# One graph layer with routed experts: an earlier closing of open blocks, an earlier first combine, the routing three slots sooner, and 112 block places

## The chip, the cores and the metric

The kernel runs on one core of a Trainium2 chip. Its time is device microseconds from start to end of one launch; the median of three runs is 1729.33 us (1729.07 to 1730.34). A separate execution was recorded by the hardware profiler. All durations of instructions come from that one.

The core has a matmul engine (PE, with its weight loads shown as PEld), three engines for elementwise work (DVE, ACT, POOL) and SP, which here only issues DMAs. Each engine works through its own instructions in program order. DMAs issued by SP form one ordered list of issues, and the indirect DMAs (gathers and scatters by a list of row numbers) are issued by POOL.

## The reference

Input: 6250 nodes with 256 features, 100000 edges sorted by destination, 16 experts. All float32.

```
xn  = layernorm(x)
gnn: h = xn @ W; deg = segment_sum(ew, dst) + 1; dinv = rsqrt(deg)
     agg = segment_sum(dinv[src]*ew*dinv[dst] * h[src], dst) + dinv^2 * h + b
     gnn = relu(0.5*(layernorm(agg)*gamma + beta) + 0.5*xn)
mix: q, k = elu(xn Wq^T)+1, elu(xn Wk^T)+1;  v = xn Wv^T      (8 heads of 32)
     mix = (q (k^T v) / max(q . sum(k), 1e-6)) Wproj^T + bproj
x   = x + gnn + mix
ffn: z = layernorm(x); top 2 of 16 experts by z @ gate_w + gate_b; softmax of the two
     moe = sum over the two of w * (relu(z @ w1[e] + b1[e]) @ w2[e] + b2[e])
x   = x + layernorm(z + moe)*gamma2 + beta2
```

So every node is sent to two experts: 12500 rows for the expert network, whose weights are 512 KB (w1) and 512 to 642 KB (w2 with biases) for one expert.

## The kernel before

**Tiles and slots.** The nodes form `NT` = 49 tiles of 128. X stays in SBUF. The order of the work is written by a loop over *slots* at the end of `windowed_layer`. Slot `c` (0 to 781) issues the gather of the 128 source rows of edge chunk `c` (line 1269, POOL), builds its one-hot matrix `hot` (line 1273, DVE), and six slots later (`LAG`) multiplies the two on PE (line 1282). All other work is cut into generators. `weave.add(at, piece)` puts one into a queue by slot, `yield n` puts the rest of it n slots later. A slot is thus a place in the program order of every engine, not a time.

**What is woven in, in this order.** `attend(t)` computes the attention's sums (slots up to 159). `residual` of a tile pair follows its edges: it finishes the two branches, updates X and computes the routing logits, over 20 slots. After each group of tiles in `PHASES`, `route(a, b, lo, hi, ...)` picks the two experts of each token, gives each token a row ("slot") in `xslots`, and lists the blocks of 128 rows that are now full. `scatter` then writes the normalised tokens to `xslots` (line 974, POOL, two scatters a tile; the norms are ACT's at line 963, in four places named `token`). Each listed block becomes one `expert` piece: SP loads w1, the block's rows and w2; PE transposes (line 1045), first product (1055), second product (1065); DVE or ACT adds the bias; SP stores the block to `yslots`. `sync` at line 1002 is the issuer of nearly all these DMAs.

**Blocks not yet full.** An expert's last block is open until it fills. At one phase (`part`) the open blocks that this phase did not fill up are closed and listed although they are not full. In the last phase `close` lists all remaining open blocks, in the order in which they were opened. The pieces of blocks are fixed in the program: `hi` says how many blocks are listed after each phase, `USUAL` how many in all. Which expert and which rows a block has is read from the list at run time (the `rows` registers on SP).

**The combine.** `combine` takes two tiles: POOL gathers four times 128 rows from `yslots` (line 1111), ACT normalises X again (1120), DVE weighs and adds (1127), takes the statistics (319, 320), normalises (1135) and adds X (1138, or 1140 and 1141 where the sum with beta was not prepared by `shift`, line 1096); SP stores the output. `LIMITS` holds pairs (tile, block): tiles below the first number have all their rows in blocks below the second, so the gather waits for the store of that block and not for all stores. The combine of a pair is placed no sooner than the slot where that block's store stands (`stored_at`).

**The guard.** `usual` is multiplied by a test at each listing: at least `hi` blocks are full, at most `FIRST` after the closing, and each pair of `LIMITS` and `USUAL` hold. If it ends at zero, the last part of the program (`again`) runs all blocks and combines once more.

**Places.** Buffers in SBUF are lent by `Places`: `spare(t)` is Q's tile t, free once the residual has read it (`read`). `got` (14 places) holds gathered rows, `w1` and `w2` have four places each, `more` holds the sums of `shift`.

The slot arithmetic of the kernel before gives, around its end: the last gather at slot 781; the residuals of the last three tiles from slots 781 and 791; routing of the last phase from 815; listed blocks 81 to 87 from slots 799 to 823 in steps of four; the last 26 blocks, 88 to 113, from slots 829 to 929; combines from slot 835 (tiles 0 and 1) in steps of five to 958.

## Time and profile before

| what | value |
|---|---|
| median of three runs | 1729.33 us |
| profiled execution, its own time | 1475.86 us |
| its span, first to last instruction | 1473.9 us |
| mean granted TensorE clock | 0.942 |
| busy: PE, PEld, DVE, ACT, POOL | 1245.1, 986.9, 914.2, 513.2, 965.5 us |
| gathers of edge rows (line 1269) | 782, 971 ns each |
| scatters of tokens (line 974) | 98, 1026 ns each |
| gathers of expert rows (line 1111) | 98, 1015 ns each |
| last gather of edge rows is issued at | 1217.5 us |
| first and last gather for the combine | 1299.2 and 1454.3 us |
| last store of a block is issued at | 1443.4 us |
| bytes moved | 353.71 MB, mean 240 GB/s |

The profiled execution is 253.5 us shorter than the median. Its span and its own time differ by 2 us. A row of the profile names line, engine, operation, and written and read tiles. "PE busy" counts modelled ends of pipelined matmuls. In tables of stretches each row gives the stretch, its length, busy time and number of instructions of each engine, the granted clock, the share of DMA time and the rate of bytes.

### The profile page before, as it was taken

Reading aid. Unit: us, or ns where it says so; the run is one execution under the profiler, and the core shown is the slowest. Engines: PE = TensorE matmul, PEld = TensorE weight load, DVE = VectorE, ACT = ScalarE, POOL = GpSimd, SP = SyncE. Lnnn points to the kernel's source line nnn. Section 1 sums busy time; section 2 is a strip of 40 time slices with the busy share of each in tenths; the row PEclk is TensorE's granted clock in tenths of the full one; section 3 lists DMA queues with packets and bytes.
Section 4 is the critical chain, followed back from the end, with each engine's and each line's share of the span. In section 5 each row is a group of like instructions: output and inputs, shape, how many; then the busy total and the mean of one; then the engine's idle time right before and its main releaser. Section 6 shows DMA issues by size and latency. Waiting matters only on the chain. (4 is left out here: it accounts for less than half of the span.)

```text
span 1473.9 us, 24429 instructions
## 1 busy us (share of the span) xinstructions
PE 1245.1 (84%) x6958; PEld 986.9 (67%) x6958; DVE 914.2 (62%) x3277; ACT 513.2 (35%) x1379; POOL 965.5 (66%) x999
## 2 busy tenths in 40 slices
PE   4879999989967787989989899797988998977880
PEld 3836666666645676877778787686867886866760
DVE  8853444457977474575745657465565456578885
ACT  3753344433332232322223232232332333345551
POOL 1007777777767777777777777777777773167634
PEclk9999999998977999999999899998999999999995
DMA  9879943333334677767878687787777887989993
GB/s 272 295 235 375 384 148 97 104 99 110 109 105 159 226 241 253 268 226 265 269 245 269 226 269 262 241 282 233 234 241 250 285 284 255 310 279 386 376 325 106
DMA packets 176777, 353.71 MB, mean 240 GB/s; under 512 B 26753, under 2 KB 115876, under 8 KB 176626
## 3 DMA queue, kind: packets, MB, share of 16 engines
q1 hardware_dynamic: 128646, 222.97, 43.7%
q0 software_dynamic: 47712, 128.17, 27.5%
q8 instruction: 62, 1.02, 0.3%
q10 hardware_dynamic: 268, 0.82, 0.2%
q14 instruction: 89, 0.73, 0.1%
HBM read 277.46 MB, written 74.38 MB: 239 GB/s over the span
## 5 line engine op out<-in xcount | busy, mean ns | idle before, releaser
L1269 POOL DMA_INDIRECT rows<-w_hs,src_t x782 | 759.6, 971 | 335.5 <-issue 92.3
L1282 PE MATMUL acc<-rows,hot 128*128 128x256 f32 x1564 | 445.4, 401 | 69.6 <-DMA rows<-w_hs,src_t 58.3
L1282 PEld LDWEIGHTS acc<-rows,hot 128*128 128x128 f32 x1564 | 278.9, 198 | 138.7 <-issue 56.1
L1273 DVE TENSOR_SCALAR hot<-iota_g,loc_t,w_t 128x128 f32<-128x128 f32 x782 | 244.7, 354 | 15.0 <-PE acc L1282 14.4
L974 POOL DMA_INDIRECT w_xslots<-Q,slot_i x98 | 100.5, 1026 | 77.6 <-ACT hT L1061 39.0
L1065 PE MATMUL yp<-early,hT 128*128 128x256 f32 x592 | 142.4, 384 | 2.2 <-ACT hT L1061 2.2
L1111 POOL DMA_INDIRECT Q<-w_yslots,slot_i x98 | 99.5, 1015 | 65.6 <-DVE xn L1127 20.1
L1061 ACT ACTIVATE hT<-hp,early 128x128 f32<-128x128 f32 x296 | 84.2, 367 | 160.5 <-PE hp L1055 116.8
L1055 PEld LDWEIGHTS hp<-Q,early 128*128 128x128 f32 x992 | 124.3, 199 | 6.2 <-ACT Q L1049 3.3
L1055 PE MATMUL hp<-Q,early 128*128 128x128 f32 x992 | 126.6, 283 | 2.1 <-ACT Q L1049 1.9
L1065 PEld LDWEIGHTS yp<-early,hT 128*128 128x128 f32 x592 | 111.8, 192 | 18.5 <-ACT hT L1061 3.7
L1049 ACT COPY Q<-xtp 128x256 f32<-128x256 f32 x114 | 42.1, 369 | 212.4 <-PE xtp L1045 211.1
L1291 DVE SCALAR_TENSOR_TENSOR agg<-acc,dinv,agg 64x256 f32<-64x256 f32 x135 | 65.1, 482 | 76.2 <-PE acc L1282 73.2
L1055 PE MATMUL hp<-Q 128*128 128x128 f32 x832 | 107.7, 286 | 0.1
L1055 PEld LDWEIGHTS hp<-Q 128*128 128x128 f32 x832 | 105.6, 202 | 2.7 <-ACT Q L1049 0.5
L569 DVE SCALAR_TENSOR_TENSOR row<-two_a,two_b 128x256 f32<-128x256 f32 (+1 forms) x49 | 21.0, 429 | 132.3 <-ACT two_b L567 132.3
L563 PE MATMUL kq<-early,xnT 128*128 128x512 f32 (+1 forms) x196 | 98.3, 625 | 4.4 <-ACT xnT L559 4.4
L1074 DVE TENSOR_TENSOR Q<-yp,early 128x256 f32<-128x256 f32 x61 | 25.8, 423 | 112.9 <-PE yp L1065 112.7
L1065 PE MATMUL yp<-Q,hT 128*128 128x256 f32 x320 | 78.3, 388 | 3.2 <-ACT hT L1061 3.2
L325 ACT ACTIVATE sd<-mv,eps_t 128x2 f32<-128x2 f32 (+2 forms) x76 | 22.7, 299 | 160.7 <-DVE mv L320 155.0
L566 ACT ACTIVATE two_a<-kq 128x512 f32<-128x512 f32 (+1 forms) x49 | 29.3, 597 | 119.3 <-issue 92.6
L1065 PEld LDWEIGHTS yp<-Q,hT 128*128 128x128 f32 x320 | 60.6, 195 | 12.8 <-ACT hT L1061 4.8
(302 smaller groups left out, 1810.5 us busy)
## 6 DMA issues: line engine op xcount, KB each, us to landing
early<-in_experts SPq DMA_DIRECT2D x61, 642.0 KB
early<-in_experts SPq DMA_DIRECT2D x62, 512.0 KB
Q<-in_experts SPq DMA_DIRECT2D x52, 512.0 KB
Q<-in_experts SPq DMA_DIRECT2D x27, 642.0 KB
w_xslots<-zero_b SPq DMA_DIRECT2D x16, 1024.0 KB
w_yslots<-zero_b SPq DMA_DIRECT2D x16, 1024.0 KB
Q<-w_xslots SPq DMA_DIRECT2D x114, 128.0 KB
w_yslots<-Q SPq DMA_DIRECT2D x114, 128.0 KB
```

The lines of the kernel that those rows point to most:

```text
L563: nc.tensor.matmul(kq[:r], xnT[:, k, :r], wkq[:, k, :], start=(k == 0), stop=(k == 1))
L566: act(e[:r].rearrange("p a c -> p (a c)"), kq[:r], AF.Exp)
L974: i = nc.gpsimd.indirect_dma_start(out=xslots, out_offset=IndirectOffsetOnAxis(ap=slot_i[:r, t, k:k + 1], axis=0), in_=y[:r], in_offset=No ...
L1049: nc.scalar.copy(xT, tp[:, :2, :])
L1055: nc.tensor.matmul(hp[:, f, :], w1[:, c, f * P:(f + 1) * P], xT[:, c, :], start=(c == 0), stop=(c == 1))
L1061: act(hT[:, f, :], hp[:, f, :], AF.Relu, bias=b1[:, f:f + 1], scale=1.0)
L1065: nc.tensor.matmul(yp[:, :D], hT[:, f, :], w2[:, f, :], start=(f == 0), stop=(f == FJ - 1 and not as_row))
L1111: g = nc.gpsimd.indirect_dma_start(out=got[i, k]()[:r], out_offset=None, in_=yslots, in_offset=IndirectOffsetOnAxis(ap=slot_i[:r, t, k:k + ...
L1269: nc.gpsimd.indirect_dma_start(out=hrows[c], out_offset=None, in_=hs, in_offset=IndirectOffsetOnAxis(ap=src_t[:, c:c + 1], axis=0))
L1273: v.tensor_scalar(hots[c], iota_g[:, group_of(c) % 2, :], loc_t[:, c:c + 1], w_t[:, c:c + 1], op0=OP.is_equal, op1=OP.mult)
L1282: nc.tensor.matmul(accs[g], hots.pop(c), hrows.pop(c), start=begin, stop=end)
L1291: v.scalar_tensor_tensor(agg(t)[p0:p1], acc[p0:p1, :], dinv[p0:p1, t:t + 1], agg(t)[p0:p1], op0=OP.mult, op1=OP.add)
```

## The change

- `PHASES` gets one more end, 44; the counts of listed blocks are a table, `LISTED`, in place of a formula: 9, 16, 24, 30, 39, 46, 55, 69, 76, 84, 87, 94 where it was 7, 15, 23, 31, 39, 47, 55, 63, 81, 88, 94.
- The closing of open blocks is at tile 36 (`CLOSING`), formerly 40, and takes only those opened before tile 28 (`CUT`, formerly 36 in its use as a limit). `LIMITS` becomes (28, 76), (36, 98), (40, 106), (46, 109), formerly (36, 85), (40, 100), (46, 110). `USUAL` falls from 114 to 112 blocks.
- `RES`, the slots between the last residual of a phase and its routing, falls from 24 to 21.
- Blocks listed at tile 36 or later stand six slots apart up to slot 773, then four (formerly: those listed at tile 40 six, later ones four).
- The first combine stands at slot `NCH + LAG + 1` = 789, with steps of 12 until the last listing and of 5 after it. Its two result tiles lie in the space of the gathered edge rows (`both`, six places, usable when the last edge product has been placed); they are finished in place and stored from there, where a tile `row` was used.
- `f_gamma` and `f_beta` are loaded at slot 762 into Q's tiles 9 and 10, formerly at slot 815 into `par`. The sums of `shift` lie in the ring of `agg`, for 10 tiles in place of 16. The scatter of the last phase uses the `token` places like the others.

By the same slot arithmetic: listed blocks 76 to 83 stand at slots 762 to 794, 84 to 86 at 798 to 806, routing of the last phase at 812, the last 25 blocks, 87 to 111, at 826 to 922; combines at 789, 801, 813, 825, 837 and then every five slots to 882 (tiles 26 and 27), from 890 for tiles 28 to 35, 922 for 36 to 39, 934 for 40 to 45, and 949 and 954 for the last three tiles.

```diff
--- before.py
+++ after.py
@@ -118,14 +118,15 @@
 
 
 
-PHASES = (8, 12, 16, 20, 24, 28, 32, 36, 40, 46, NT)
-CUT = 36
-AFTER = PHASES.index(CUT) + 1
-FIRST, USUAL = 2 * PHASES[AFTER] + 5, 2 * NT + 16
-LIMITS = ((CUT, FIRST), (PHASES[AFTER], 2 * NT + 2), (PHASES[-2], 2 * NT + 12))
+
+PHASES = (8, 12, 16, 20, 24, 28, 32, 36, 40, 44, 46, NT)
+LISTED = (9, 16, 24, 30, 39, 46, 55, 69, 76, 84, 87, 94)
+CUT, CLOSING = 28, 36
+FIRST, USUAL = 76, 2 * NT + 14
+LIMITS = ((CUT, FIRST), (36, 98), (40, 106), (46, 109))
 MOST = P
 
-RES = 24
+RES = 21
 WA = 2 * F
 WB = WROW - D
 
@@ -737,7 +738,7 @@
 
     s = state("s")
 
-    opened = {t: one([P, 1], f"opened{t}") for t, _ in LIMITS[1:]}
+    opened = {t: one([P, 1], f"opened{t}") for t, _ in LIMITS}
 
     def top2(a, b):
 
@@ -827,6 +828,7 @@
         if part:
             old = small("old")
             v.scalar_tensor_tensor(old, whole, 0.0, s["had"], op0=OP.is_equal, op1=OP.mult)
+            v.scalar_tensor_tensor(old, s["open"], opened[CUT], old, op0=OP.is_lt, op1=OP.mult)
 
             few = small("few", 1)
             v.tensor_reduce(few, old, axis=AX.X, op=OP.add)
@@ -962,7 +964,7 @@
             r = rows(t)
             act(places[t]()[:r], X[:r, t, :], AF.Identity, bias=nm2[:r, t:t + 1], scale=rs2[:r, t:t + 1])
 
-        first = len(homes[kind].free) if kind == "got" else 4
+        first = 4
         for t in range(a, min(b, a + first)):
             norm(t)
             yield 1
@@ -1099,10 +1101,11 @@
     def combine(ts_, homes, pool, last):
 
         n = len(ts_)
-        mv = pool.tile([P, n, 2], F32, name="mv", bufs=3)
-        rs = pool.tile([P, n], F32, name="rs", bufs=3)
+        mv = pool.tile([P, n, 2], F32, name="both_mv", bufs=3)
+        rs = pool.tile([P, n], F32, name="both_rs", bufs=3)
         v.memset(mv, 1.0)
-        both = pool.tile([P, 2, D], F32, name="xn2", bufs=3)
+        home = homes["both"].take()
+        both = home().rearrange("p (i c) -> p i c", i=2)
         got, ys = {}, []
         for i, t in enumerate(ts_):
             r = rows(t)
@@ -1133,13 +1136,14 @@
         for i, t in enumerate(ts_):
             r, y = rows(t), ys[i]
             v.scalar_tensor_tensor(y[:r], y[:r], mv[:r, i, 0:1], last[:r, 0, :], op0=OP.subtract, op1=OP.mult)
-            o = pool.tile([P, D], F32, name="row", bufs=3)
             if t in shifted:
-                v.scalar_tensor_tensor(o[:r], y[:r], rs[:r, i:i + 1], shifted[t]()[:r], op0=OP.mult, op1=OP.add)
+                v.scalar_tensor_tensor(y[:r], y[:r], rs[:r, i:i + 1], shifted[t]()[:r], op0=OP.mult, op1=OP.add)
             else:
                 v.scalar_tensor_tensor(y[:r], y[:r], rs[:r, i:i + 1], last[:r, 1, :], op0=OP.mult, op1=OP.add)
-                v.tensor_add(o[:r], y[:r], X[:r, t, :])
-            sync(out[t * P:t * P + r, :], o[:r])
+                v.tensor_add(y[:r], y[:r], X[:r, t, :])
+            sync(out[t * P:t * P + r, :], y[:r])
+            if i == n - 1:
+                homes["both"].give(home)
             yield 2
 
 
@@ -1179,7 +1183,9 @@
              "w1": Places(((), lambda: early[:, :WA]), ((), lambda: early[:, WA:2 * WA]), spare(14, 4), spare(18, 4)),
              "w2": Places(((), lambda: early[:, 2 * WA:WA + WROW]), ((), lambda: early[:, WA + WROW:]),
                           spare(22, 6), spare(28, 6)),
-             "more": Places(*[((), lambda i=i: hrow[:, i, :]) for i in range(NROW)], *[spare(t) for t in range(9, 13)]),
+             "more": Places(*[((), lambda j=j: ring[j]) for j in range(RING)], *[spare(t) for t in (11, 12)]),
+             "both": Places(*[(("rows",), lambda j=j: hrow[:, 2 * j:2 * j + 2, :].rearrange("p i c -> p (i c)"))
+                              for j in range(NROW // 2)]),
              "got": Places(*[spare(t) for t in range(35, NT)])}
 
 
@@ -1215,42 +1221,45 @@
                 if t + RING < NT and t >= 4:
                     sum_from(t + RING)
             at += 10
-        hi = 2 * b - (9 if n < AFTER else -1 if n == AFTER else 4)
+        hi = LISTED[n]
         ready = max(last_at + RES, scattered - 2)
         def routed(a=a, b=b, lo=lo, hi=hi, n=n, flush=flush):
-            yield from route(a, b, lo, hi, n == 0, n == AFTER)
+            yield from route(a, b, lo, hi, n == 0, b == CLOSING)
             if flush:
                 yield 1
                 yield from close(hi, USUAL)
         weave.add(ready, routed())
-        if flush or n == AFTER:
+        listed_at = ready + 20
+        if flush or b == CLOSING:
             weave.add(ready + 6, token_weights(*((CUT, NT) if flush else (0, CUT))))
         slow = 0 if flush else 1
-        weave.add(ready + 2, scatter(n, a, b, 9, "token" if slow else "got", slow))
+        weave.add(ready + 2, scatter(n, a, b, 9, "token", slow))
         scattered = ready + 11 + 2 * (b - a) * slow
         ready += 14 + (2 * (b - a) * slow)
         for j in range(lo, USUAL if flush else hi):
             ends[j] = hi if j < hi else USUAL
-            block = max(block + (4 if n > AFTER or block > NCH - 9 else 6 if n == AFTER else 7), ready)
+            block = max(block + (4 if block > NCH - 9 else 6 if b > 32 else 7), ready)
 
             weave.add(block, expert(n, j, homes, bank, (4, 3) if n < 3 else (5, 4), 5 if block > NCH - 18 else 2, flush))
             stored_at[j] = block + 24
         lo, a = hi, b
     def block_of(t):
         return next((limit for b, limit in LIMITS if t < b), USUAL)
-    last = par
+    last = Q[:, 9:11, :]
     def load_last():
+        assert read.issuperset((9, 10))
         nc.sync.dma_start(last[:, 0, :], bcast(f_gamma, D))
         nc.sync.dma_start(last[:, 1, :], bcast(f_beta, D))
         return
         yield
-    weave.add(last_at + RES, load_last())
-    weave.add(last_at + RES + 22, shift(range(NT - NROW - 4, NT), last))
-    at = last_at + RES
+    weave.add(NCH - 20, load_last())
+    weave.add(last_at + RES + 22, shift(range(NT - RING - 2, NT), last))
+    at = NCH + LAG + 1
     for t0 in range(0, NT, 2):
         at = max(at, stored_at[min(block_of(t0), USUAL) - 1])
         weave.add(at, combine(range(t0, min(NT, t0 + 2)), homes, mp, last))
-        at += 5
+
+        at += 12 if at < listed_at else 5
     again = []
     def load_again():
         v.tensor_scalar(usual_i, usual, 0.0, None, op0=OP.is_equal)
@@ -1290,6 +1299,8 @@
                         assert t in begun and t not in summed, (slot, t, summed_at)
                         v.scalar_tensor_tensor(agg(t)[p0:p1], acc[p0:p1, :], dinv[p0:p1, t:t + 1], agg(t)[p0:p1],
                                                op0=OP.mult, op1=OP.add)
+            if c == NCH - 1:
+                read.add("rows")
         weave.run(slot)
         slot += 1
     msg.close()
@@ -1309,7 +1320,7 @@
             return Places(*[((), lambda t=t: t) for t in tiles])
 
         homes = {"x": places(4, D, "x"), "xT": places(2, D, "xT"), "hT": places(2, F, "hT"),
-                 "y": places(2, D, "y"), "w1": places(4, WA, "w1"), "w2": places(4, WROW - WA, "w2"), "got": places(8, D, "got")}
+                 "y": places(2, D, "y"), "w1": places(4, WA, "w1"), "w2": places(4, WROW - WA, "w2"), "got": places(8, D, "got"), "both": places(4, 2 * D, "both")}
         weave = Weave()
         block = 0
         loaded.clear()
```

## The prediction

> **What bounds the kernel now.** I read the table of stretches first, then engines in order of time around the last gather of edge rows, then the waits, then the chain that ended last. The columns: stretch, length, then PE, PEld, DVE, ACT and POOL busy with their counts, clock, DMA share, GB/s.
>
> ```profile
> core 0: us, PE busy (x) PEld busy (x) DVE busy (x) ACT busy (x) POOL busy (x), PEclk, DMA share, GB/s
> 1150.00:1200.00 50.00, 49.44 (x292) 42.48 (x291) 27.38 (x81) 14.42 (x42) 38.12 (x40) 1.00 0.84 282
> 1218.00:1230.00 12.00, 8.53 (x52) 7.45 (x52) 11.17 (x52) 3.79 (x11) 1.38 (x2) 1.00 0.67 249
> 1230.00:1298.00 68.00, 60.66 (x376) 51.60 (x376) 35.10 (x160) 27.96 (x84) 18.15 (x18) 0.95 0.77 261
> 1298.00:1440.00 142.00, 113.21 (x710) 95.47 (x710) 121.21 (x348) 70.51 (x218) 86.98 (x87) 0.98 0.98 354
> 1440.00:1474.00 34.00, 0.00 (x0) 0.00 (x0) 20.19 (x57) 4.20 (x11) 12.49 (x12) 0.51 0.33 94
> ```
>
> Four stages follow from it. **Edges**, to 1217.5 us: POOL issues one gather after the other. Its 38.1 us in 50 are its ceiling, since each instruction of 0.95 us is followed by 0.30 us:
>
> ```profile
> 1216.26 0.95 POOL L1269 DMA_INDIRECT rows<-w_hs,src_t  x1 [0.30 <-PE hp L1055]
> 1217.51 0.95 POOL L1269 DMA_INDIRECT rows<-w_hs,src_t  x1 [0.30 <-PE hp L1055]
> 1229.07 1.00 POOL L974 DMA_INDIRECT w_xslots<-Q,slot_i  x1 [10.62 <-issue]
> ```
>
> The third line shows that the scatters of tiles 40 to 45 come after the last gather, when POOL has nothing else to do. **A**, 1217.5 to 1299.2 (first gather for a combine): residual of the last tiles, last routing, and blocks. PE is busy for 60.7 of 68 us, POOL for 18; DMA is at 0.77. **B**, 1299.2 to 1443.4 (last store of a block): DMA share 0.98, DVE busy 121 of 142. Both the transfers and DVE's combine are near their limit, the transfers nearer. **C**, 30.5 us: the last combine. Its chain starts with the landing of the last gather:
>
> ```profile
> 1454.28 6.09 DMA Q<-w_yslots,slot_i
> ```
>
> **The change, stage by stage.**
>
> **Edges: +10.2.** Scatters of tiles 40 to 43, eight in number, now stand at slots 749 to 757, ahead of the last 25 gathers. POOL's step is 1.27 us (0.97 + 0.30), so the last gather is issued 8 x 1.27 = 10.2 us later. They were free before. Three more blocks run in this stage (77 in place of 74, counted by the slot of their products). PE's 49.4 of 50 us at the six-slot spacing looks full, but POOL keeps its ceiling there (38.1), so PE does not hold it back; were PE full, these blocks would add 3 x 3.7 = 11 us, which overlaps with the 10.2. I take 10.2, bounds 8 and 20. One more routing (about 60 DVE instructions of 0.2 us) falls where DVE is busy 27 of 50 us: nothing, and 12 us without that cover. Longer lists, the load of gamma and beta (two SP issues of 0.45 us) and RES are nothing: three slots sooner, the routing's first DVE instruction still stands behind DVE's own logits addition, which waits for the same product.
>
> **A: -12.** PE's order decides. One block costs PE 3.7 us, from start to start:
>
> ```profile
> 1265.41 0.38 PE L1045 MATMUL xtp<-ident,Q 128*128 128x128 f32 x2
> 1265.62 1.95 PE L1055 MATMUL hp<-Q 128*128 128x128 f32 x16
> 1267.41 0.38 PE L1045 MATMUL xtp<-ident,Q 128*128 128x128 f32 x2
> ```
>
> (0.2 + 1.8, and 1.7 for the second product.) Between the slot of the last edges and the final list, 14 blocks stand before and 10 after: 4 x 3.7 = -14.9. ACT's wait disappears too:
>
> ```profile
> ACT Q L963 <- DMA w_xslots<-Q,slot_i: 10.7, 2, 9.1
> ```
>
> Six tiles in four token places made ACT wait for a scatter to land; behind it stood the copy `h`, for which DVE's statistics waited 6.4 us. The phase is now split in four and two tiles. PE idles some 5 us there: -5 (bounds 0, -9). Against it, three combines stand ahead of the final list, 12 gathers on POOL (idle) and DVE work of 6.4 us a pair:
>
> ```profile
> 1412.44 1.00 DVE L1127 SCALAR_TENSOR_TENSOR xn<-Q,w,xn 128x256 f32<-128x256 f32 x2
> 1418.90 1.00 DVE L1127 SCALAR_TENSOR_TENSOR xn<-Q,w,xn 128x256 f32<-128x256 f32 x2
> ```
>
> These are 19.3 us in an engine with 33 idle of 68. They cost nothing where the routing waits for PE and everything where it waits for DVE; behind them are the statistics of the residual and the routing, for which PE's `row` product and SP's loads wait. I take a third, +6 (bounds 0 and 19).
>
> Here a rule speaks against the change. By the Trainium skill, "TensorE: Matmul & The Clock Gate", section "What's actually happening", an idle window of about 3.4 us puts the clock at half. Fewer blocks make PE idle where it waited for the routing. The row: the longest PE waits before, 3.3 and 2.6 us, go with 0.95 over the stretch, about 3 us lost. By the row a sparser A loses nothing more; by the rule each of three pairs of 6.4 us can open one such window, an estimate of 1.7 us each, +5. I take +2. Sum: -14.9 - 5 + 6 + 2 = -12 (bounds -20 and +6).
>
> **B: -12.** It starts with eight tiles already combined (slots 789 to 825) and one block less. Per tile, two gathers and a store are 3 x 131 KB = 0.39 MB; per block the two weights, rows in and out are 1.3 MB. So 8 x 0.39 + 1.3 = 4.4 MB, at 354 GB/s -12.6 us; rows in and out of three further blocks, moved ahead of B, are about 0.5 MB, another -1.4. DVE's share falls by more (four pairs, 25.6 us), so DMA stays the limit and the other 12 us are not had. Against it, waits. The gathers of tiles 28 to 35 stand exactly at the store of block 97, those of 36, 40 and 46 at blocks 105, 108 and 111. SP's list puts the output of tile 28 at slot 901, before most loads of blocks 105 to 111, so a late gather holds weights back. From store to output: 4.2 (a store at 1427.64 released a gather at 1431.84) + 2.5 for two gathers + 6.1 landing + 6.5 for the pair = 19.3 us, against 14 slots of 1.29 us (5.15 us a block of four slots) = 18.0. The skill's "DMA: Bandwidth & Descriptors", section "Anatomy of one DMA", gives 2.0 us plus bytes by 436 GB/s for such a gather: estimate 2.3 us, path 15.5, no wait. The measured 6.1, in a loaded queue, decides: 1.3 us, taken as +2 with bounds 0 and 15. B: -12 (bounds -25, where DVE had been the limit, and +2).
>
> **C: 0.** In both kernels the last three tiles wait for the last store; six gathers, a landing, a pair and an output follow.
>
> **Sum.** 10.2 - 12 - 12 = -14 us against 1475.86: 1462, a ratio of 0.990. The median is 253.5 us above this execution, and no view shows where that lies. A fixed offset gives 1715, a scale of 1.172 gives 1713; I take 1713.
>
> **That it does what it says.** The routing's counting, followed through on the reference's inputs, leaves the guard at one in both kernels: 24 full blocks at tile 16 for 24 listed, 73 at the closing (69 to 76), 97 of 98, 103 of 106, 106 of 109, and 112 of 112 at the end. Were it zero, 128 blocks of at least 3.7 us are another 470 us. One chance in a hundred, within the slower case.
>
> **Rivals.**
> 1. *The tail is limited by work, and DVE's limit counts in B.* A gets -18, B -22: -30 us, 1699. For it: DVE at 121 of 142 us and POOL's gathers waiting for DVE. Against: DMA at 0.98.
> 2. *The last residual, routing and listing set A by their latency.* A stays as long: 10.2 + 0 - 12 = -2, 1727, no change. For it: PE waits for `code_s` twice. Against: PE's blocks run back to back from 1250 to 1282.
> 3. *Slower: the early combines delay the routing.* All three pairs' DVE time (19.3), the clock's 5 and a pair waiting for its gathers 3 us fall on the path: A = -14.9 + 27 = +12, the sum +10, 1741. It decides from A = +2 on, when early DVE work on the path exceeds about 17 us. For it: DVE takes its instructions in order, 46 of 80 us are busy already, and the flush list waits for DVE. Against: its gaps there are mostly waits for PE's block products.
>
> **How the numbers follow.** Chances: forecast 0.53 (own range 1703 to 1724), rival 1 0.17, rival 2 0.11, rival 3 0.19 with the guard. Differences under 0.2%, 3.5 us, cannot be told from none. Faster is 0.53 + 0.17 = 0.70, same 0.11, slower 0.19. To leave out no more than 2 in 10 the range takes rival 1 with most of its spread and rival 3 to its centre: 1692 to 1741.
>
> **What would show it.** Last gather of edge rows near 1228 us. First combine gathers shortly after it, in a POOL stretch that was idle. From the last edge gather to the first weight load of the last 25 blocks about 68 us, with no ACT wait at line 963. B with DMA above 0.95 and about 132 us. No repeat pass: 112 stores of blocks. The prediction is wrong if the edges lengthen by more than 20 us (then PE was full), if A does not shrink (combines on the routing's path), or if SP waits long for outputs of combines before loads (gates).

## The result, and the profile after

| | median | span of all times |
|---|---|---|
| before | 1729.20 us | 1722.54 to 1730.34 |
| changed | 1770.64 us | 1766.89 to 1776.14 |

The ratio is 1.025 (1.0212 to 1.0288): the change makes the kernel slower by 41 us. 1713 us was predicted.

One thing has to be known before two profiles are compared: the kernel before takes 1726 to 1755 us in some sessions on the chips and 1476 us in others (the same chip gave 1725.8 and later 1476.1 us), every kernel of a session shares its condition, and the profile that the prediction worked with came from a session of 1476 us while all times came from long ones. Below, "long" and "short" name these two kinds of session, and ratios are always to the kernel before in the same session. In a short session the changed kernel stands at **1.0005** (0.9992 to 1.0018), in a second long one at **1.0277** (1.0239 to 1.0315).

So the profile shown before has two counterparts. First the changed kernel in a short session (run e13), by the same stages: 50 us of edges, the first 12 us behind the last gather, the rest of A, B, C. Columns as before: stretch, length, PE, PEld, DVE, ACT and POOL busy, clock, DMA share, GB/s.

```profile
core 0: us, PE busy (x) PEld busy (x) DVE busy (x) ACT busy (x) POOL busy (x), PEclk, DMA share, GB/s
1150.00:1200.00 50.00, 48.03 (x275) 40.88 (x274) 38.19 (x150) 15.60 (x42) 38.10 (x40) 0.97 0.83 275
1231.30:1243.00 11.70, 7.25 (x23) 5.32 (x21) 5.02 (x23) 0.96 (x2) 8.96 (x10) 0.57 0.78 282
1243.00:1307.60 64.60, 44.84 (x291) 38.05 (x290) 50.10 (x194) 27.04 (x75) 27.43 (x27) 0.88 0.61 201
1307.60:1444.40 136.80, 110.16 (x675) 93.52 (x675) 102.09 (x295) 65.33 (x203) 60.12 (x61) 0.91 0.94 328
1444.40:1476.60 32.20, 0.00 (x0) 0.00 (x0) 19.63 (x57) 3.93 (x10) 9.97 (x9) 0.50 0.32 93
```

Then the kernel before in a long session (run e1), and the changed kernel's profile of the result, long too:

```profile
core 0: us, PE busy (x) PEld busy (x) DVE busy (x) ACT busy (x) POOL busy (x), PEclk, DMA share, GB/s
1250.00:1300.00 50.00, 43.59 (x222) 35.01 (x223) 24.90 (x85) 15.76 (x42) 31.75 (x33) 0.93 0.66 217
1471.00:1544.50 73.50, 63.50 (x394) 54.19 (x393) 38.68 (x174) 29.21 (x88) 19.32 (x18) 0.95 0.70 240
1544.50:1710.10 165.60, 118.31 (x713) 97.46 (x711) 125.25 (x360) 71.67 (x223) 89.98 (x90) 0.92 0.89 309
```

```profile
core 0: us, PE busy (x) PEld busy (x) DVE busy (x) ACT busy (x) POOL busy (x), PEclk, DMA share, GB/s
1250.00:1300.00 50.00, 42.75 (x222) 36.18 (x223) 25.44 (x99) 14.61 (x40) 27.46 (x30) 0.90 0.67 224
1489.00:1571.00 82.00, 56.32 (x338) 47.45 (x338) 63.62 (x267) 30.51 (x85) 29.68 (x28) 0.85 0.61 200
1571.00:1737.00 166.00, 117.77 (x675) 96.54 (x675) 100.34 (x289) 64.63 (x203) 61.85 (x64) 0.83 0.81 274
```

Then A from the last row gather to the first x load of the closing list, before and changed, both short (the same columns):

```profile
1217.50:1296.00 78.50, 68.65 (x427) 58.91 (x428) 46.74 (x214) 32.15 (x96) 20.02 (x19) 0.96 0.76 264
1231.30:1307.60 76.30, 52.09 (x313) 43.37 (x311) 55.12 (x217) 28.00 (x77) 36.38 (x36) 0.84 0.64 213
```

The reader is to see three things. In the edge stage POOL no longer keeps the 38 us in 50 that the prediction called its ceiling once the session is long: 32 and 27 us. In A, PE's work shrinks as predicted (68.65 to 52.09 us) and the stretch hardly does (78.5 to 76.3). In B, the DMA share falls below what it was before (0.94 for 0.98 in the short session, 0.81 for 0.89 in the long one).

Stage by stage, from the times at which the last row gather, the first x load of the closing list and the last block store are issued (the prediction's A is measured here to that x load). An x load fetches a block's rows; the closing list is the one written by the last routing, 25 or 26 blocks:

| us | Edges, last gather at | A | B | C | span |
|---|---|---|---|---|---|
| before, short | 1217.5 | 78.4 | 147.5 (26 blocks) | 30.5 | 1473.9 |
| changed, short (e13) | 1231.3 | 76.3 | 136.8 (25) | 32.2 | 1476.6 |
| difference | +13.8 | -2.1 | -10.7 | +1.7 | +2.7 |
| predicted | +10.2 | -12 | -12 | 0 | -14 |
| before, long (e1) | 1458.6 | 85.8 | 165.7 (26) | 33.7 | 1743.8 |
| changed, long (result) | 1477.3 | 93.3 | 166.2 (25) | 33.3 | 1770.1 |
| difference | +18.7 | +7.5 | +0.5 | -0.4 | +26.3 |

The two long profiles are from different sessions (medians of before 1729 and 1754), so their difference is smaller than the result's 41 us. Within the session of e1 stand three near relatives of the changed kernel, e2 to e4 below. Against e1 their last gather comes 22.6 to 33.2 us later, A is 5.2 to 10.6 us longer, B 1.0 to 12.0, and C changes by 1.0 at most. So the Edges are the largest part of the long loss. A single profile is no finer than that: two of the changed kernel, the result and e5, differ by 5.4 us at the last gather and by 8.3 in B.

POOL's time behind the last gather, idle before, is now filled in part (POOL's timeline of the changed kernel, long, with rows left out between the first two pairs):

```profile
1473.50 0.95 POOL L1114 DMA_INDIRECT Q<-w_yslots,slot_i  x1 [0.30 <-issue]
1477.26 0.94 POOL L1278 DMA_INDIRECT rows<-w_hs,src_t  x1 [0.30 <-issue]
1486.00 0.95 POOL L1114 DMA_INDIRECT Q<-w_yslots,slot_i  x1 [0.30 <-issue]
1497.32 1.00 POOL L976 DMA_INDIRECT w_xslots<-Q,slot_i  x1 [10.37 <-issue]
```

The first combine gathers even stand ahead of the last gather of edge rows (four of them, at 1471.0 to 1474.8), and by the first x load of the closing list 29 of them have been issued. The first token scatter behind the last row gather (line 976) comes 20.1 us after it here, and 10.0 us after it in e13. 112 blocks are stored: there is no repeat pass.

### The profile page after: what moved, and what is told of

Its sections match the earlier page's. It is cut to its first block, busy times and chain, and to the rows that moved or that the text cites. A ratio compares the mean times of both kernels' runs of the same rounds, so it can differ in the third digit from the quotient of the medians.

```text
span 1770.1 us, 24312 instructions
## 1 busy us (share of the span) xinstructions
PE 1311.2 (74%) x6911; PEld 1029.3 (58%) x6911; DVE 920.4 (52%) x3353; ACT 510.4 (29%) x1368; POOL 963.6 (54%) x999
## 5 line engine op out<-in xcount | busy, mean ns | idle before, releaser
L1291 PEld LDWEIGHTS acc<-rows,hot 128*128 128x128 f32 x1564 | 292.6, 204 | 75.0 <-issue 20.7
L1067 PE MATMUL yp<-early,hT 128*128 128x256 f32 x584 | 171.8, 446 | 118.5 <-ACT hT L1063 99.9
L1067 PEld LDWEIGHTS yp<-early,hT 128*128 128x128 f32 x584 | 125.6, 223 | 153.5 <-ACT hT L1063 111.8
L1057 PE MATMUL hp<-Q,early 128*128 128x128 f32 x976 | 130.5, 291 | 25.4 <-issue 14.3
L1057 PEld LDWEIGHTS hp<-Q,early 128*128 128x128 f32 x976 | 126.1, 205 | 32.2 <-issue 17.4
L1067 PE MATMUL yp<-Q,hT 128*128 128x256 f32 x312 | 92.0, 447 | 59.4 <-ACT hT L1063 52.9
L1067 PEld LDWEIGHTS yp<-Q,hT 128*128 128x128 f32 x312 | 66.6, 224 | 77.6 <-ACT hT L1063 59.6
L564 PE MATMUL kq<-early,xnT 128*128 128x512 f32 (+1 forms) x196 | 99.6, 632 | 13.6 <-ACT xnT L560 10.2
L1063 ACT ACTIVATE hT<-hp,Q 128x128 f32<-128x128 f32 x156 | 44.6, 370 | 115.2 <-remote 47.6
L698 PE MATMUL mix<-M,two_b 128*128 128x256 f32 (+1 forms) x196 | 61.4, 441 | 19.6 <-ACT two_b L656 19.5
```

Source lines behind the costliest of these rows:

```text
L564: nc.tensor.matmul(kq[:r], xnT[:, k, :r], wkq[:, k, :], start=(k == 0), stop=(k == 1))
L698: nc.tensor.matmul(mix[:r0, i, :], qT[:, k, i * P:i * P + r0], M[:, k, :], start=(k == 0), stop=False)
L1057: nc.tensor.matmul(hp[:, f, :], w1[:, c, f * P:(f + 1) * P], xT[:, c, :], start=(c == 0), stop=(c == 1))
L1063: act(hT[:, f, :], hp[:, f, :], AF.Relu, bias=b1[:, f:f + 1], scale=1.0)
L1067: nc.tensor.matmul(yp[:, :D], hT[:, f, :], w2[:, f, :], start=(f == 0), stop=(f == FJ - 1 and not as_row))
L1291: nc.tensor.matmul(accs[g], hots.pop(c), hrows.pop(c), start=begin, stop=end)
```

## The experiments

Each run's ratio is to the kernel before in its own session. Runs e1 to e4 were in a long session (before 1753.8 us), e5 to e8 in a long one (1725.8), e9 to e12 in a short one (1476.2), e13 to e16 in a short one (1476.1), e17 and e18 in a long one (1755.5).

### First four: the place of the difference (long)

**e1: the kernel before, again**, for a profile that belongs to its times.

> The kernel before, unchanged, to see where its 1729 us lie: its one profile so far is 253 us shorter. Theory 1 (the long runs are longer in the edge stage): about 1729 us, and a profile whose last gather of edge rows is issued near 1440 us instead of 1217.5, while the rest, from there to the end, stays near 256 us. Theory 2 (all stages stretch alike): last gather near 1430 us and a tail of about 300 us. If the profile is again near 1476 us, the difference is between recorded and unrecorded executions.

Measured 1752.99 us, ratio 0.9996 (0.9968 to 1.0024), profile 1745.8 us. The long time is what this kernel takes throughout such a session. Of the 270 us between the two profiles 241 lie in the edge stage and 29 behind it, so neither theory's numbers are met. 40 gathers take 58 to 79 us through most of the edge stage, where the short profile has 50 to 62, while the first gather stands at 106 to 107 us in both.

**e2: routing 24 slots behind the residual.**

```diff
-RES = 21
+RES = 24
```

> The changed kernel with the routing again 24 slots behind its residual (the three slots are undone, nothing else). If the earlier routing makes DVE wait for its residual, about 1729 us to 1750 us; if the three slots are free, as the prediction had it, 1770 us within 4 us.

Measured 1.0147 (1.0101 to 1.0193). But its stages stand where the changed kernel's do: last gather 1481.2, A 96.4, B 166.7. It is the lowest of the three of its session (e3 1.0271, e4 1.0213), which points to a gain, but without the changed kernel beside it the ratio alone proves little; e11 repeats it.

**e3: the first combine at the last routing.**

```diff
-    at = NCH + LAG + 1
+    at = last_at + RES
...
-        at += 12 if at < listed_at else 5
+        at += 5
```

> The changed kernel with the first combine back behind the last routing's slot (812, steps of five), nothing else undone. The rival of the prediction (early combines delay the last routing) expects 1740 to 1750 us. If the early combine gains what the prediction gave it, slower than 1770 us by 5 to 15. If the loss lies in the edge stage, 1765 to 1785 us, and the last gather of edge rows stays within 5 us.

Measured 1.0271 (1.0237 to 1.0306), A 91.0 us. This edit did not do what it was for: 22 combine gathers were still issued before the closing list's first x load (29 in the changed kernel), so it decides nothing. e9 goes further.

**e4: blocks listed at tile 36 seven slots apart.**

```diff
-            block = max(block + (4 if block > NCH - 9 else 6 if b > 32 else 7), ready)
+            block = max(block + (4 if block > NCH - 9 else 6 if b > 36 else 7), ready)
```

> The changed kernel with the 14 blocks listed at tile 36 seven slots apart instead of six. If closer blocks lengthen the edge stage because each block waits for its weights, 1750 to 1760 us and a last gather of edge rows 10 to 20 us sooner. If the spacing is free, 1770 us within 5 us.

Measured 1.0213 (1.0175 to 1.0251). 74 blocks instead of 76 are stored ahead of the last gather, and the stretch from edge gather 700 (of 782) to the last is 144.7 us, where the changed kernel has 148 to 150. A gain of 4 us at most, and the tail is no shorter (296.9 us from the last gather to the end; the changed kernel's result has 292.8): not the cause.

### Second four: one part undone, one part alone (long)

**e5: the changed kernel again**, as the anchor of its session.

> The changed kernel as it is, run beside the three below, so that each of them can be set against it. If the first result carries over, 1.02 to 1.03 of the kernel before, with the last row gather some 15 to 20 us later than before's and the last stage (first x load of the closing list to last block store) no shorter though it has one block less.

Measured 1774.10 us, 1.0277 (1.0239 to 1.0315): the result repeats.

**e6: the changed kernel without the routing at tile 44.**

```diff
-PHASES = (8, 12, 16, 20, 24, 28, 32, 36, 40, 44, 46, NT)
-LISTED = (9, 16, 24, 30, 39, 46, 55, 69, 76, 84, 87, 94)
+PHASES = (8, 12, 16, 20, 24, 28, 32, 36, 40, 46, NT)
+LISTED = (9, 16, 24, 30, 39, 46, 55, 69, 79, 87, 94)
```

> The changed kernel without the routing at tile 44 (tiles 40 to 45 are routed together at 46, with a list of 87, and their twelve token scatters stand behind the last row gather again); all else as changed. Theory 1, the scatters and the routing of tile 44 in the last quarter of the edge stage are what makes the stage longer: the last gather comes about 19 us sooner (from about 1477 to about 1460 us) and the ratio to before falls by about 0.010, less whatever the six scatter places more behind the last gather (8 x 1.27 us = 10 us) cost in the routing that follows. Theory 2, the stage is longer because of the combines or of the longer lists: last gather within 5 us of the changed kernel's, ratio within 0.004.

Measured 1.0269 (1.0220 to 1.0318): no gain. The gain in the edges is there (gather 700 to the last 137.7 us for 150.0), but A takes 8.5 of these 12.3 us back (102.4 for 93.9) and B as much again (166.4 for 157.9): 18 scatters instead of 10 now stand behind the last gather, among the combine gathers. (This profile is of an execution 15 us below the median of its kernel.)

**e7: the kernel before with the routing at tile 44 and nothing else.**

```diff
-PHASES = (8, 12, 16, 20, 24, 28, 32, 36, 40, 46, NT)
+PHASES = (8, 12, 16, 20, 24, 28, 32, 36, 40, 44, 46, NT)
```

> The kernel before with one more routing, at tile 44 with a list of 84, and nothing else. Theory 1: its last gather comes 10 (eight scatters at 1.27 us) to 19 us (as between the two profiles) later than before's, and the time rises by about as much less what the routing behind the last gather saves: ratio 1.003 to 1.010. Theory 2: last gather within 5 us of before's, ratio 0.997 to 1.003.

Measured 1.009 (1.0043 to 1.0137), with 139.5 us from gather 700 to the last for 130.7 in e8: +8.8, near the prediction's 10.2 for eight scatters. This part alone is a loss. A is 74.1 us for 80.8 in e8, so A gives 6.7 back.

**e8: the kernel before with 111 places and nothing else.**

```diff
-FIRST, USUAL = 2 * PHASES[AFTER] + 5, 2 * NT + 16
-LIMITS = ((CUT, FIRST), (PHASES[AFTER], 2 * NT + 2), (PHASES[-2], 2 * NT + 12))
+FIRST, USUAL = 2 * PHASES[AFTER] + 5, 2 * NT + 13
+LIMITS = ((CUT, FIRST), (PHASES[AFTER], 2 * NT + 1), (PHASES[-2], 2 * NT + 8))
```

> The kernel before with 111 places of blocks for 114 (and the two limits behind which tiles wait at 99 and 106 for 100 and 110), and nothing else: three blocks less in the closing list. By the prediction's working, where a block in that list costs 354 GB/s worth of its two weights or 5.2 us of pace, 3 blocks are worth 11 to 16 us: ratio 0.991 to 0.994. If the end of the kernel is set by the gates of the combines and not by the blocks' weights, under 5 us: ratio over 0.997.

Measured 0.9968 (0.9945 to 0.9991): three blocks less are worth 5.4 us, 1.8 us each and not the 3.6 to 5.2 that was expected. B is 150.8 us for 23 blocks, but C grows to 39.9: with fewer blocks the combines of the last tiles come out at the end instead.

### Third four: from the changed kernel back, step by step (short)

Each of these keeps the edits of those before it.

**e9: the combines' places behind the closing list.**

```diff
-    at = NCH + LAG + 1
+    at = listed_at + 3
...
-        at += 12 if at < listed_at else 5
+        at += 5
```

> The changed kernel with no combine listed ahead of the closing list: all of them start 3 slots behind the place where the routing has written it, five slots apart, as in the kernel before; nothing else is undone. (The earlier late start still left 22 combine gathers ahead of the closing list's first x load.) Theory 1, the early combines delay the last residuals and the last routing: the time from the last row gather to the first x load of the closing list falls from 93 us to 74 to 80 us (74 is what the kernel before has with tile 44 routed by itself), the edge stage stays as it is, and the stage of the closing list grows by less than half of that, since it has only one block less to cover 28 tiles more: ratio to before 1.013 to 1.020. Theory 2, the combines only fill time in which the routing waits anyway, and another part of the change makes the stretch long: it stays within 5 us of 93 us, the closing list gets longer by the combines' time, and the ratio is 1.03 or more.

**e10: and no routing at tile 44** (the edit of e6).

> The kernel of the run before this one, with the routing at tile 44 taken out too. Added to the kernel before alone, it cost 0.9%; taken from the changed kernel alone it gave nothing. If it costs 0.9% wherever no early combine stands in the way of the last routing, the ratio falls by 0.006 to 0.010 against the run before this one, with the last row gather 9 to 12 us sooner and the stretch behind it 7 to 10 us longer. If not, it stays within 0.004.

**e11: and `RES` 24** (the edit of e2).

> The kernel of the run before this one, with every routing 24 slots behind its residual again instead of 21. If routing sooner costs time by itself (on another chip, the changed kernel with 24 stood at 1.0147 of before, and with 21 at 1.0277 on this kind of run), the ratio falls by 0.006 to 0.013; if the difference was the chip's, it stays within 0.004 and no stage moves by more than 4 us.

**e12: and the old lists and closing.**

```diff
-LISTED = (9, 16, 24, 30, 39, 46, 55, 69, 79, 87, 94)
-CUT, CLOSING = 28, 36
-FIRST, USUAL = 76, 2 * NT + 14
-LIMITS = ((CUT, FIRST), (36, 98), (40, 106), (46, 109))
+LISTED = (7, 15, 23, 31, 39, 47, 55, 63, 81, 88, 94)
+CUT, CLOSING = 36, 40
+FIRST, USUAL = 85, 2 * NT + 14
+LIMITS = ((CUT, FIRST), (40, 100), (46, 110))
...
-            block = max(block + (4 if block > NCH - 9 else 6 if b > 32 else 7), ready)
+            block = max(block + (4 if b > 40 or block > NCH - 9 else 6 if b == 40 else 7), ready)
```

> The kernel of the run before this one, with closing at tile 40, the old lists (63, 81 and 88 blocks by tiles 36, 40 and 46 for 69, 79 and 87) and the old distances of blocks. What is left of the change is 112 places of blocks and the combines' own buffers. Theory: the two blocks that the changed lists put ahead of the last row gather (76 for 74) and their distance of 6 slots cost the edge stage 4 to 8 us; with the old ones the last gather comes so much sooner, and the ratio is 0.996 to 1.000, that of 112 places alone. If the lists cost nothing, the ratio is that of the run before this one.

| | ratio | last gather | gather 700 to last | A | B | C |
|---|---|---|---|---|---|---|
| e9 | 1.0031 (1.0018 to 1.0045) | 1226.8 | 117.4 | 71.6 | 144.1 | 34.8 |
| e10 | 1.0010 (0.9995 to 1.0025) | 1217.8 | 107.4 | 76.9 | 144.4 | 32.4 |
| e11 | 0.9978 (0.9966 to 0.9991) | 1216.2 | 104.9 | 76.2 | 143.5 | 32.1 |
| e12 | 1.0007 (0.9992 to 1.0023) | 1220.5 | 104.0 | 78.7 | 143.3 | 38.6 |

One thing in e9 to e11, and in every later run with their combines, is not as the edit reads: 14 combine gathers are still issued ahead of the closing list's first x load. POOL's program does not keep the order of slots, and tiles 0 to 27 wait only for the first 76 blocks there. So the edit takes away 15 of the changed kernel's 29. (e12, whose first tiles wait for 85 blocks, has none.)

Tile 44's routing costs the edges 10.0 us (e9 less e10, from gather 700 on; the prediction had 8 x 1.27 = 10.2) and gives 5.3 us back in A. Three slots sooner cost 3.8 us (medians 1476.19 and 1472.40), 2.5 of them in the edge stage; the prediction had put them at nothing. e11 less e12 shows what closing at tile 36 and the longer lists are worth by themselves: -5 us, a gain. The two more blocks that e11 has ahead of the last gather cost that stage 0.9 us at most, next to nothing as predicted.

e12 and e11 also try the step on which the prediction's A rests. With the old lists PE is busy for 70.36 us of A, with the new ones for 61.90, and A shortens by 2.5 us (e11, then e12):

```profile
1216.20:1292.40 76.20, 61.90 (x337) 50.44 (x336) 47.09 (x212) 26.31 (x76) 34.79 (x33) 0.84 0.66 229
1220.50:1299.20 78.70, 70.36 (x428) 59.96 (x428) 45.91 (x210) 30.92 (x93) 19.64 (x19) 0.93 0.75 259
```

### Fourth four: early combines and gates on one chip (short)

**e13: the changed kernel; e14: the kernel of e9; e15: the kernel of e11; e16: e15 with tighter gates** (a gate: the number of blocks whose stores a tile's combine waits for).

```diff
-LIMITS = ((CUT, FIRST), (36, 98), (40, 106), (46, 109))
+LIMITS = ((CUT, FIRST), (36, 97), (40, 103), (46, 106))
```

> The changed kernel as it is, beside the next run, on one chip. Theory 1, the early combines are what loses: ratio at least 0.010 above the next run's, with the stretch from the last row gather to the closing list's first x load some 15 to 20 us longer (on a chip where the kernel before takes 1476 us, where everything waits less, at least 8 us and 0.005). Theory 2, what differed between the runs so far was the chip and not the kernel: the two ratios agree within 0.004 and the stretches within 5 us.

> The changed kernel with all combines listed behind the closing list, once more, now beside the changed kernel as it is. Theory 1: stretch behind the last gather of 72 to 80 us, ratio 1.003 (as on the chip with 1476 us) to 1.015. Theory 2: the changed kernel's ratio within 0.004.

> The changed kernel with the combines behind the closing list, without the routing at tile 44, and with routing 24 slots behind its residual. It was at 0.9978 on the chip with 1476 us. What it keeps is closing at tile 36, the longer lists and 112 places. 0.995 to 1.000 if these three are a gain on any chip; over 1.003 if on a chip with 1730 us the two or three blocks ahead of the last gather cost more than they save behind it.

> The kernel of the run before this one, with the gates of the combines at 97, 103 and 106 blocks for 98, 106 and 109: tiles 36 to 39 wait for three blocks less and tiles 40 to 45 as well. If the gates hold up the end of the kernel, as the prediction's two gate terms have it, 2 to 6 us less than the run before this one (0.002 to 0.004); nothing if the last block and the combines of the last tiles set the end anyway.

Measured: e13 1.0005 (0.9992 to 1.0018), e14 1.0027 (1.0006 to 1.0047), e15 0.9964 (0.9949 to 0.9978), e16 0.9935 (0.9907 to 0.9963). In a short session the 15 early gathers that e14 lacks are not a loss: A is 2.8 us longer with them (76.3 for 73.5), B 7.3 shorter (136.8 for 144.1). The theory that they are what loses falls for this kind of session. Tighter gates gain 2.7 us in the medians, but the intervals of e15 and e16 overlap and the two profiles don't differ (1468.3 and 1469.3): not established.

### Last two: the same question in a long session

**e17: the kernel of e9 and e14; e18: the kernel of e16.**

> The changed kernel with all combines behind the closing list, a third time, for a session in which the kernel before takes some 1730 to 1750 us. Where it takes 1476 us, this kernel is at 1.003 and the changed one at 1.0005. Theory 1, in a long session the early combines are what loses: the stretch from the last gather to the closing list's first x load comes down from 94 us to under 82, the ratio from 1.026 to 1.015 or less. Theory 2, it is the longer edge stage and the gaps of PE that lose there: the stretch stays over 88 us, the ratio over 1.020. If the session is one of 1476 us, 1.003 again and nothing is decided.

> Combines behind the closing list, no routing at tile 44, routing 24 slots behind its residual, gates at 97, 103 and 106 blocks, once more, beside the run before this one. It was at 0.9935 of the kernel before where that takes 1476 us. There again: 0.991 to 0.998. Where the kernel before takes 1730 us: 0.990 to 1.000 if it has lost what made the changed kernel slower there, over 1.010 if closing at tile 36 with the longer lists is itself what loses there.

Measured: e17 1.0114 (1.0043 to 1.0186), e18 0.9979 (0.9953 to 1.0005). With 15 of the 29 early gathers gone, more than half of the loss is gone (1.0277 and 1.025 for the changed kernel in two other long sessions). The ratio is the one that theory 1 named, the stretch isn't: A is 87.5 us, neither under 82 nor over 88, for 93.9 in e5, and B **145.3 for 157.9**, so most of it went in B, which no theory on record had said. e18 has an edge stage as short as before's (130.2 us from gather 700 to the last; e1 129.4), so what is left of the loss in e17 lies in what e18 drops, tile 44 and `RES` (its tighter gates gained nothing that e16 could establish), and closing at tile 36 with the longer lists loses nothing there either. How tile 44 can cost 8.8 us in e7 and about 18 with the changed lists (e2 against e18, which differ in their combines and sessions too; 12.3 from e5 to e6, in one session) stays open.

### What a long session does, and why B loses there

First A. It grows with the combine gathers that are issued ahead of the closing list's first x load; in us:

| Combine gathers ahead of the list | 0 | 14 | 22 to 30 |
|---|---|---|---|
| short, routing at tile 44 | | 71.6, 73.5 (e9, e14) | 76.3 (e13) |
| short, no routing at 44 | 78.4, 78.7 (before, e12) | 75.0 to 76.9 (e10, e11, e15, e16) | |
| long, routing at tile 44 | 74.1 (e7) | 87.5 (e17) | 91.0 to 96.4 (result, e2 to e5) |
| long, no routing at 44 | 80.8, 85.8 (e8, e1) | 95.0 (e18) | 102.4 (e6) |

In a long session 14 early gathers go with 9 to 14 us, 22 to 30 of them with 17 to 22; in a short one with less than 5 us. The kernels of the first column have the old lists too, but those put more blocks into A and not fewer. The first scatter behind the last row gather shows the delay at its beginning: 10.9 us after it in e7, 19.9 to 20.2 in e5, e17 and the result, with seven combine gathers between; with the same seven it is 10.0 in e13 and e14.

Then B, and how a long session slows. SP's list of DMA issues shows it. In B, the eight tiles 28 to 35 wait for block 97; when its store lands, POOL issues their 16 gathers without a pause, 1.25 us apart. SP's timeline during that run, changed kernel, long (e5; POOL's run goes from 1650.87 to 1670.85):

```profile
1651.05 0.35 SPq L1004 DMA_DIRECT2D out_dram<-rows  x1
1652.14 0.01 SPq L1004 DMA_DIRECT2D w_yslots<-Q  x1
1652.27 0.62 SPq L1004 DMA_DIRECT2D early<-in_experts  x1
1653.65 0.01 SPq L1004 DMA_DIRECT2D early<-w_b2rows  x1
1655.07 0.02 SPq L1004 DMA_DIRECT2D out_dram<-rows  x1
1657.99 0.69 SPq L1004 DMA_DIRECT2D early<-in_experts  x1
1660.11 0.02 SPq L1004 DMA_DIRECT2D Q<-w_xslots  x1
1662.94 0.71 SPq L1004 DMA_DIRECT2D w_yslots<-Q  x1
1665.78 0.00 SPq L1004 DMA_DIRECT2D Q<-in_experts  x1
1667.87 0.70 SPq L1004 DMA_DIRECT2D Q<-w_b2rows  x1
1670.67 0.00 SPq L1004 DMA_DIRECT2D out_dram<-rows  x1
1673.48 0.00 SPq L1004 DMA_DIRECT2D early<-in_experts  x1
1673.60 0.33 SPq L1004 DMA_DIRECT2D Q<-w_xslots  x1
1674.17 0.36 SPq L1004 DMA_DIRECT2D w_yslots<-Q  x1
```

Within the same run of 16 gathers in the same kernel, short (e13, part of it):

```profile
1387.92 0.36 SPq L1004 DMA_DIRECT2D w_yslots<-Q  x1
1388.53 0.33 SPq L1004 DMA_DIRECT2D Q<-in_experts  x1
1389.12 0.30 SPq L1004 DMA_DIRECT2D Q<-w_b2rows  x1
1389.85 0.35 SPq L1004 DMA_DIRECT2D out_dram<-rows  x1
1390.44 0.34 SPq L1004 DMA_DIRECT2D early<-in_experts  x1
1390.97 0.36 SPq L1004 DMA_DIRECT2D Q<-w_xslots  x1
```

In the long session SP gets 11 issues off in 20 us, from 1655 us on one in 2.1 to 2.9 us, and is back at one in 0.6 us less than 3 us after POOL's last gather; in the short one it makes 22 in 19.5 us. It is not the DMA issues alone that slow. SP's small instructions between them, register moves, additions and semaphore waits, take 0.70 us in 8 of 12 cases from 1661.5 to 1672.8 us (a move takes 0.03 us in the short profile). PE slows too, in the middle of a block's first product (its timeline, e5):

```profile
1662.80 1.97 PE L1057 MATMUL hp<-Q 128*128 128x128 f32 x8
1665.81 0.37 PE L1057 MATMUL hp<-Q 128*128 128x128 f32 x1 [1.04 <-issue]
1667.20 0.37 PE L1057 MATMUL hp<-Q 128*128 128x128 f32 x1 [1.02 <-issue]
1667.93 0.55 PE L1057 MATMUL hp<-Q 128*128 128x128 f32 x1 [0.36 <-issue]
```

The first eight matmuls start 0.2 to 0.3 us apart, the rest of this product 0.7 to 2.8 us, and no wait shows in between. It is not for want of what SP had issued before: no packet of SP's DMAs runs between 1663.0 and 1666.0 us, so the earlier ones had been moved and the queue was dry. ACT's hidden layer of this block begins when the run is over (its timeline, e5):

```profile
1673.71 1.14 ACT L1063 ACTIVATE hT<-hp,early 128x128 f32<-128x128 f32 x4 [13.84 <-remote]
```

What ended ACT's wait isn't told. The stores of blocks 97 to 100 are issued at 1646.4, 1652.1, 1662.9 and 1674.2, against 1376.4, 1381.7, 1387.9 and 1392.0: 27.8 us for three blocks, 15.6 in the short profile. In e17 no such run occurs there: POOL's gathers take turns with DVE.

```profile
1645.93 1.07 POOL L1114 DMA_INDIRECT Q<-w_yslots,slot_i  x1 [1.19 <-DVE rows L1130]
1647.30 0.94 POOL L1114 DMA_INDIRECT Q<-w_yslots,slot_i  x1 [0.30 <-DVE rows L1138]
```

The last blocks' stores follow each other at 5.2 us in e17 and at 5.85 in e5 (first to last store of the closing list, over the number of steps). Over all long profiles they come 5.85 to 6.17 us apart in the six that have this run of 16 gathers (the result, e2 to e6), and 5.18 to 5.29 in the five that don't (e1, e7, e8, e17, e18). In the short e13, with the same run, it is 4.99. That the run does it was not isolated: e1 and e7 have runs of 19 and 20 gathers at the head of B, and there, and in e8 without such a run, it is the list's first store that comes late (36 to 39 us after the first x load, 17 to 23 in the short profiles).

Counted over the program (runs of eight or more indirect DMAs at most 1.5 us apart, from 250 us on, without the first 2 us of each): SP makes 0.39 to 0.42 issues a us inside such runs in the four short profiles counted (before, e9, e13, e15), with a median of 0.6 us from one to the next, and 0.15 to 0.20 in the five long ones (e1, result, e5, e17, e18), 1.4 to 1.9 us apart. Outside the runs the medians are 0.60 to 0.61 and 0.71 to 0.76. The register moves say the same without any DMA in them: in the short four none of some 480 takes more than 0.04 us; in the long five 25 to 48 in a hundred take 0.5 us or more inside the runs, and 6 to 8 in a hundred outside. PE's slow steps are rarer: of the steps from one matmul to the next within a block's first product, 2 to 3 in a hundred are longer than 0.8 us inside the runs of e1, the result and e5, none in those of e17 and e18, and none anywhere in before, e9 and e13.

The indirect DMAs themselves cost the same on POOL. The groups of edge gathers, before short and before long (e1):

```profile
L1269 POOL DMA_INDIRECT rows<-w_hs,src_t x782 | 759.6, 971 | 335.5 <-issue 92.3
```

```profile
L1269 POOL DMA_INDIRECT rows<-w_hs,src_t x782 | 762.6, 975 | 574.9 <-PE acc L1282 172.9
```

971 and 975 ns each, and 239 us more idle. The transfers are not slower either: SP's DMA packets took 43.7% of 1473.9 us before short and 37.6% of 1743.8 before long, 644 and 656 us. So a long session stretches waits and SP's small instructions, and neither POOL's gathers nor the transfers. SP's moves and additions of 0.3 us or more sum to 56 to 77 us in a long profile, so by their own time they don't make up the 253. What does, and what brings a session into one condition or the other, is unknown. The long profiles also hold fewer than half of the semaphore records (13511 for 32532), so the names of releasers in them ("remote", "issue") can't be relied on.

## Why the prediction was wrong

**The sum over its own profile: -14 predicted, +2.7 measured in the same condition. The step that failed is A.** "PE's order decides. One block costs PE 3.7 us ... 4 x 3.7 = -14.9." PE's work did fall, from 68.65 us between the last gather and the closing list's x load to 52.09, by 16.6. PE's idle time rose from 9.9 to 24.2 us, so the stretch got only 2.1 us shorter. In e11 against e12 it is the same: 8.5 us less for PE, 2.5 us less of A. What PE waits for there, in the changed kernel (waits from 1231.3 to 1316 us, e13):

```profile
PE xtp L1047 <- DMA Q<-w_xslots: 11.6, 2, 6.6
PE row L945 <- DVE code_s L942: 7.5, 1, 7.5
PE row L903 <- DVE code_s L899: 5.8, 1, 5.8
```

These are the routing (`code_s`, on DVE) and the first rows of the list that it writes. Between 1288 and 1316 us PE is busy for 3.1 us and DVE for 22.8. From the last row gather to the last scatter there are 71.7 us before and 69.6 after, and the first x load follows the last scatter by 6.7 us in both. So this chain of residual, routing and scatters sets A. Which of its steps is the long one was not isolated; in its first part, from 1244 to 1274 us, PE is still busy for 28.95 us of 30. That is rival 2, "the last residual, routing and listing set A by their latency", with -2 us forecast: +2.7 in the short profiles, 1.0005 by the times. The rival's evidence stood in the prediction itself (PE waits for `code_s`), and was outweighed by a view of PE at 60.7 of 68 us. A busy engine in a stretch is not yet its limit.

**The -5 for ACT's wait** named the right thing: no wait of ACT for a scatter is left in that stretch. None of it can be seen in A's length. **The +6 for early combines** was about right in a short session (A is 2.8 us longer with 29 early gathers than with 14). **The +2 for the clock** can't be read off: the granted clock over A fell from 0.96 to 0.84 (e13), further than the row of the long PE waits had suggested and toward the rule that had been given less weight, but on an engine that no longer sets the stretch.

**Edges, +10.2, measured +13.8.** The eight scatters are 10.0 us (e9, e10). Most of the missing part is `RES`, put at nothing because "the routing's first DVE instruction still stands behind DVE's own logits addition"; e11 measured 2.5 us in this stage and 3.8 in all; why is not shown. That PE would not hold POOL back was right in the short session and no longer true in the long one.

**B, -12, measured -10.7**: the right size, and luck in part. The bytes fell by more than was forecast (346 GB/s over 147.5 us are 51.0 MB, 328 over 136.8 are 44.9, a difference of 6.1 for some 5; the forecast's own 0.5 MB for rows of three blocks should have been 6 x 131 KB = 0.8), but the rate fell with them, and the list's stores come 4.99 us apart for 4.96. What B gained is one block less and a first store 16.9 us behind the first x load for 23.3. The early combines take 7.3 us out of B (e13 against e14). They run up against the gates, though; POOL's waits from 1300 us on, e13:

```profile
POOL Q L1114 <- DVE rows L1130: 48.5, 26, 19.9
POOL Q L1114 <- DMA w_yslots<-Q: 20.9, 1, 20.9
```

20.9 us for the store of block 105, for which tiles 36 to 39 wait and behind them all later ones. The 19.9 are put down to DVE, but end 5.3 us after the issue of block 97's store, much as the other ends 4.8 us after that of block 105: the gate of tiles 28 to 35. From there on the end is the 13 tiles' own time, 53.6 us from the first of their gathers to the end of the program, whatever was combined earlier. **C, 0, measured +1.7.** Gates were given +2 with a bound of 15.

**The step from 1475.86 us to the median failed as well.** "A fixed offset gives 1715, a scale of 1.172 gives 1713": both suppose that the 253 us lying in no view have nothing to do with the change. They have. A long session slows SP, and at times PE, beside POOL's runs of gathers, and the change adds to these runs: eight scatters within the edge stage, 25 combine gathers in A where there were none (POOL busy there 36.5 us in e5, 20.3 in e1), and the 16 gathers in a row at the gate of block 97. From gather 700 to the last the changed kernel takes 148.1 to 150.0 us, e1 and e8 129.4 and 130.7: a loss of some 20 us in this part of the Edges, where the forecast had 10.2. In A the early combines go with not 6 us but 13 to 22 (e7 at 74.1 us, e17 at 87.5, the changed kernel and its near relatives at 91.0 to 96.4), so A gets longer and not shorter. B's gain shrinks or goes: 157.9 and 166.2 us for e1's 165.7, with a block less. These differences are measured, between kernels that differ in lists and `RES` too; that the slowing of SP and PE causes them is argued from the traces alone. Rival 3 had the sign, +10 by early combines delaying the routing, and 19 in a hundred; A bears it out in a long session, but the Edges lose more than A, and more of what e17 gives back lies in B.

**The range**, 1692 to 1741, took in no case in which the 253 us themselves change with the edit.

**The best version measured.** e16 and e18, the same kernel, at 0.9935 (0.9907 to 0.9963) short and 0.9979 (0.9953 to 1.0005) long: it keeps closing at tile 36, the longer lists and 112 places, and drops tile 44, the three slots and 15 of the 29 early gathers. In the long session its interval still touches no change against the kernel before.

## What to carry to other kernels

Before a profile's stretches are summed up, its own time has to be one that the kernel is measured at: if it isn't, the time that no view explains may be the one that the change alters. And work taken off an engine that is busy for 90% of a stretch shortens it only if no chain of dependent steps runs through the whole stretch; follow that chain from its first to its last instruction and compare its length first. Gathers that one gate releases all at once, or that fill an idle stretch ahead of a dependent chain, are not free because POOL was idle: in the long sessions here they went with slower issues of SP and a longer chain.

## What had not been expected of the hardware

- The same program, one core, takes 1476 or 1726 to 1755 us, by session and not by chip, with the mean clock at 0.93 to 0.94 and 0.87 to 0.90. POOL's gathers last the same (971 and 975 ns), and so do SP's transfers in sum (644 and 656 us); waits are longer, and some of SP's register moves take 0.5 to 1.1 us in place of 0.03.
- In the long sessions SP's DMA issues slow from one in 0.6 us to one in 1.4 to 1.9 us (median) while POOL issues indirect DMAs back to back; in the run shown they recover within 3 us of its last, and PE's matmuls of one product, 0.7 to 2.8 us apart beside it, with them.
- POOL's instructions do not stand in the order of slots: combine gathers written for slots from 789 on came before the row gathers of slots 780 and 781.
